# Attention's preparation rearranged: second batch's v computed inside the attention, its norm in steps between rotations, head 0's float16 pairs on other engines

## The chip, the cores and the metric

The program runs on one core of a Trainium2 chip. A core has five engines, each with its own in-order queue, which meet only at semaphores: PE (TensorE, matrix products), DVE (VectorE), ACT (ScalarE), POOL (GpSimd) and SP (SyncE, which here only issues DMAs). The metric is the device time of one execution in microseconds, with the median of several executions as the time of a kernel.

## The reference

Four layers run one after the other on an image batch x of shape (2, 128, 64, 64): an attention block, a block with deformable convolutions, three steps of a convolutional network, and a state space block. Only the first, layer 0, is touched here:

```python
# b=2, c=128, L=64*64=4096, 4 heads of ch=32 channels
xn = (xg - mean) * jax.lax.rsqrt(var + EPS)          # group norm, var with ddof=1
xi = (xn * gn_w + gn_b)                               # (b, c, L)
qkv = jnp.einsum('oc,bcl->bol', w_qkv, xi) + b_qkv[None, :, None]
q, k, v = jnp.split(jnp.transpose(qkv, (0, 2, 1)), 3, axis=2)
q = _apply_rotary(pos, q)
k = _apply_rotary(pos, k)
weight = jnp.einsum('bct,bcs->bts', qh * scale, kh * scale)   # per batch and head, L x L
weight = jax.nn.softmax(weight.astype(jnp.float16), axis=-1)
a = jnp.einsum('bts,bcs->bct', weight, vh).reshape(b, c, L)
hout = jnp.einsum('oc,bcl->bol', w_proj, a) + b_proj[None, :, None]
return (xi + hout).reshape(b, c, h, w)
```

## The kernel before

Channels lie on the 128 partitions, the 4096 pixels along the free dimension. The pixels are cut into `NBLK` = 8 blocks of `BLK` = 512. Layer 0 (function `layer0`) has two stages.

**Preparation.** x of both batches is loaded into the two tiles `q4[0]` and `q4[1]`, the rotary cosines and sines into `cs` (block by block, `load_cs`). All orders of work between `with tc.manual_schedule()` and its end are those of the program text: every engine executes its instructions in the order in which the loop issues them.

- `group_norm(b)`: eight `bn_stats` on DVE (L168), their aggregate (L170), two small matmuls with `grp` which sum over groups (L75, L82, in `group_affine`), a square root on ACT (L84), four small operations on DVE (L86 to L92), and eight ACT instructions that write the normalised image into `g.xa` (L176).
- The loop over n = 0 to 15 is batch b = n // 8, block k = n % 8. In each n, `rotated(b, k, j)` runs for q (j = 0) and k (j = 1): four PE passes into a PSUM tile `pq` (L183; three buffers), two DVE operations that multiply by cosine and sine (L185, L187, into `rt1` and `rt2`, two buffers each), an addition on POOL (L189, into `rt3`, pool `cp`, five buffers), and a store to DRAM by SP (L190, to `qd` or `kd`). The function returns the reduction of the block's largest magnitude (L191), which the loop issues one rotation later, from the list `due`.
- `values(b, k)` follows in each n: 16 PE matmuls (L199) give v of that block in PSUM (pool `psg`, two buffers). It is stored as three bfloat16 parts whose sum is the float32 value, by ACT (L204, L206, L208) and POOL (L207, L209), in `v3[b]`.
- `group_norm(1)` stands after n = 4, so batch 1 is normalised while batch 0 is still being rotated.
- At n = 10 SP loads k of head 0 (four copies, from `kd[0]`) into `q4[1]`, whose x is no longer needed, and the first two pieces of q into staging tiles (`fetch`, pool `stg`, two buffers). At n = 12 to 14 `split` turns them into float16 pairs: a float16 copy on ACT (L287), and on DVE the differences to it for some of the partitions (L289). The pairs of a head lie in `qk[0]` or `qk[1]`, which are the bytes of `q4[0]` and `q4[1]`.

After the loop the largest magnitudes become a flag (L244 to L260), each engine reads it, and a branch chooses `attend` (taken here) or `attend_any`.

**Attention** (`attend`). A unit is a batch, a head, a block `qb` of 512 queries and a block `kb` of 128 keys. Units run in groups of `GR` = 3: three score matmuls into a PSUM tile `ps` of three banks (L312; two buffers), one exp on ACT for all three (L318), and, `LAG` = 2 groups later, three matmuls that add the weighted v into `acc` (L328). `acc` comes from the pool `psa`, which has two buffers of one bank[...]. When the last key block of a query block is in, `normalise` reads `acc` on DVE (L339 reciprocal, L340 and L341 copies, L345 three products) and POOL adds the three parts (L346, L347). After the last head, `project` takes a bank of `psa` too (L354, L356). Pieces of later heads are fetched at `kb` 4 and split at `kb` 26, the copy on POOL and the differences on DVE.

Of the kernel before, what the change touches and what calls it, by code (L numbers as in the profile page):

```python
# [10 lines left out]
F32 = mybir.dt.float32  # L11
# [16 lines left out]
NH = 4  # L28
CH = P // NH
# [23 lines left out]
def interior(g, b, r0=0, rows=HW):  # L53
    return g.xa[:, b, 1 + r0 : 1 + r0 + rows, 1 : 1 + HW]
# [16 lines left out]
def group_affine(g, sm, ps_tile, mv, grp, gamma, beta, eps, unbias):  # L71


    nc = g.nc
    nc.tensor.matmul(ps_tile[:, 0:1], grp, mv[:, 0:1], start=True, stop=True)  # L75
    mg = sm.tile([P, 1], F32, name="ga_mg")
    nc.vector.tensor_copy(mg, ps_tile[:, 0:1])
    dm = sm.tile([P, 1], F32, name="ga_dm")
    nc.vector.tensor_sub(dm, mv[:, 0:1], mg)
    vt = sm.tile([P, 1], F32, name="ga_vt")  # L80
    nc.vector.scalar_tensor_tensor(vt, dm, dm, mv[:, 1:2], ALU.mult, ALU.add)
    nc.tensor.matmul(ps_tile[:, 1:2], grp, vt, start=True, stop=True)  # L82
    sd = sm.tile([P, 1], F32, name="ga_sd")
    nc.scalar.activation(sd, ps_tile[:, 1:2], AF.Sqrt, bias=eps, scale=unbias)  # L84
    rs = sm.tile([P, 1], F32, name="ga_rs")
    nc.vector.reciprocal(rs, sd)  # L86
    sc = sm.tile([P, 1], F32, name="ga_sc")
    nc.vector.tensor_mul(sc, rs, gamma)
    tm = sm.tile([P, 1], F32, name="ga_tm")
    nc.vector.tensor_mul(tm, mg, sc)  # L90
    sh = sm.tile([P, 1], F32, name="ga_sh")
    nc.vector.tensor_sub(sh, beta, tm)  # L92
    return sc, sh


def flat(ap):
    return ap.rearrange("p r w -> p (r w)")

# [1 line left out]
def layer0(g, I):  # L100
# [5 lines left out]
    nc, tc = g.nc, g.tc  # L106
    with ExitStack() as ctx:
        w = ctx.enter_context(tc.tile_pool(name="l0w", bufs=1))
        dr = ctx.enter_context(tc.tile_pool(name="l0dr", bufs=1, space=bass.MemoryType.DRAM))
        wv = w.tile([P, P], F32, name="wv")  # L110
        nc.scalar.dma_start(wv, I["wvT"])
        wpt = w.tile([P, P], F32, name="wpt")
# [14 lines left out]
        with ExitStack() as pctx:  # L127
# [20 lines left out]
            def load_cs(k):  # L148
                nc.sync.dma_start(cs[:, k], I["cossin"][:, :, k * BLK : (k + 1) * BLK])

            for k in range(4):
                load_x(0, k)
            for k in range(3):
                load_cs(k)
            for k in range(4):
                load_x(1, k)
                load_cs(3 + k)
            load_cs(7)
            bv = pw.tile([P, 1], F32, name="bv")
# [4 lines left out]
            def group_norm(b):  # L164

                st = sm.tile([P, NBLK, 6], F32, name="st")
                for k in range(NBLK):
                    nc.vector.bn_stats(st[:, k, :], q4[b][:, k * BLK : (k + 1) * BLK])  # L168
                mv = sm.tile([P, 2], F32, name="mv")
                nc.vector.bn_aggr(mv, st.rearrange("p k s -> p (k s)"))  # L170
                pg = psg.tile([P, BLK], F32, name="pm")
                n = float(P // 4 * L)
                sc, sh = group_affine(g, sm, pg, mv, grp, vec(g, "gn_w"), vec(g, "gn_b"), g.eps6, n / (n - 1.0))
                for k in range(NBLK):
                    x = img(q4[b][:, k * BLK : (k + 1) * BLK])
                    nc.scalar.activation(interior(g, b, k * RB, RB), x, AF.Identity, bias=sh, scale=sc)  # L176

            def rotated(b, k, j):

# [14 lines left out]

            def values(b, k):
                pv = psg.tile([P, BLK], F32, name="pm")
                for r in range(RB):
                    half = slice(64 * (r % 2), 64 * (r % 2) + 64)
                    nc.tensor.matmul(  # L199
                        pv[half, r // 2 * P : (r // 2 + 1) * P], g.xa[:, b, 1 + k * RB + r, 1 : 1 + HW], wv,  # L200
                        start=True, stop=True,
                    )
                v32 = sm.tile([P, 4, NH, CH], F32, name="v32")
                nc.scalar.copy(v32.rearrange("p c h d -> p (c h d)"), pv)  # L204
                dst = v3[b][:, 4 * k : 4 * k + 4]
                nc.scalar.copy(dst[:, :, :, 0:CH], v32)  # L206
                nc.gpsimd.tensor_sub(v32, v32, dst[:, :, :, 0:CH])  # L207
                nc.scalar.copy(dst[:, :, :, CH : 2 * CH], v32)  # L208
                return lambda: nc.gpsimd.tensor_sub(dst[:, :, :, 2 * CH : 3 * CH], v32, dst[:, :, :, CH : 2 * CH])  # L209

            with tc.manual_schedule():
                due = []
                group_norm(0)
                for n in range(NB * NBLK):
                    b, k = divmod(n, NBLK)
                    for j in range(2):
                        f = rotated(b, k, j)
                        for f0 in due:
                            f0()
                        due = [f]  # L220
                    due.append(values(b, k))

                    if n == 4:
                        group_norm(1)
                    if n == NBLK + 2:
                        for r in range(4):
                            nc.sync.dma_start(q4[1][r * CH : (r + 1) * CH, :], kd[0][0:CH, :])
                        first = [fetch(g, stg, qd, 0, c) for c in range(2)]
                    elif NBLK + 4 <= n < NBLK + 6:
                        for c in range(2 * (n - NBLK - 4), 2 * (n - NBLK - 4) + 2):  # L230
                            split(g, qk[0], 1, c, q4[1][:, c * PIECE : (c + 1) * PIECE], nc.scalar.copy)
                    elif n == NBLK + 6:
                        for c in range(2):
                            split(g, qk[0], 0, c, first[c], nc.scalar.copy)
                for f0 in due:
                    f0()
# [28 lines left out]
        with cond.Else():  # L265
            attend_any(g, v3, wp3, bo, qd, kd, q4)


# [12 lines left out]
    return t  # L281


def split(g, qk, j, c, t, copy):

    dst = qk[:, j, c * PIECE : (c + 1) * PIECE]
    copy(dst, t)  # L287
    for p0, p1 in ((64, 128),) if j else ((32, 64), (96, 128)):
        g.nc.vector.tensor_sub(dst[p0:p1], t[p0:p1], dst[p0:p1])  # L289


def attend(g, v3, wpt, bo, qd, kd, qk, stg):


    nc, tc = g.nc, g.tc
# [3 lines left out]
    with ExitStack() as ctx:  # L299
# [23 lines left out]
        def weigh(group, e):  # L323
            nonlocal acc
            for i, (b, h, qb, kb) in enumerate(group):
                if kb == 0:
                    acc = psa.tile([P, BLK], F32, name="acc")
                nc.tensor.matmul(acc, v3[b][:, kb, h, :], e[:, i, :], start=(kb == 0), stop=(kb == NS - 1))  # L328
# [39 lines left out]
        ]  # L368
        held, done, coming = [], [], []
        with tc.manual_schedule():  # L370
            for u in range(0, len(units), GR):
                group = units[u : u + GR]
                b, h, qb, kb = group[0]
                held.append((group, scores(group)))
                if done and 24 <= kb < 24 + GR:
                    project(*done.pop(0))
                if len(held) > LAG:
                    weigh(*held.pop(0))
                if 4 <= kb < 4 + GR:
                    coming = [(n, j, c, fetch(g, stg, (qd, kd)[j], n, c)) for n, j, c in pieces(b * NH + h, qb)]  # L380
                elif 26 <= kb < 26 + GR:
                    for n, j, c, t in coming:
                        split(g, qk[n % 2], j, c, t, nc.gpsimd.tensor_copy)
# [1636 lines left out]
```

## Time and profile before

| what | value |
|---|---|
| median of 3 runs | 5577.32 us (5575.88 to 5578.47) |
| time of the profiled execution | 5576.86 us |
| its span | 5574.9 us |
| preparation: span's start to first score matmul | 134.54 us |
| attention: first to last score group | 134.5 to 1062.6 us |
| PE busy, whole span | 4717.5 us, 85% |
| DVE busy | 4540.1 us, 81% |
| ACT busy | 4087.5 us, 73% |
| POOL busy | 3642.2 us, 65% |
| L318 exp | 683 instructions, 919.0 us busy |
| L312 and L328 | 2048 matmuls each, 554.0 and 553.6 us busy |

Engines work beside each other, so shares of busy time do not add up, and an average over the whole span says little about one stage: what a change in a stage is worth is read from the instructions of that stage and from what each of them waited for. In the lines of the profile `L185` is a line of the kernel, `out<-in` names the tile written and the tiles read, `xN` a number of instructions merged into one line, and a bracket the idle time of the engine before it with the instruction that ended it. Matmul durations overlap (they are pipelined), so their pitch, not their sum, is the time PE takes. The granted clock of PE is given as a share of full speed.

### The profile page before, as it was taken

What the parts mean: (1) busy time and instruction counts of PE and PEld (TensorE: products, weight loads), DVE (VectorE), ACT (ScalarE), POOL (GpSimd) and SP (SyncE); (2) the same over time, 40 slices, a digit from 0 to 9 for tenths busy, and PEclk for the clock granted to TensorE, in tenths of its full rate; (3) what the DMA queues carried; (4) which work ended last, traced back from release to release, by engine and by line L of the source; (5) the groups of instructions that cost most, each with busy time, mean ns of one, the idle gap of its engine ahead of it and who ended that gap; (6) DMA issues with size and microseconds to landing.
All of it is one profiled execution on the core that took longest, in us unless ns stands there. A gap on an engine that the chain in (4) does not pass through costs nothing.

```text
span 5574.9 us, 54509 instructions
## 1 busy us (share of the span) xinstructions
PE 4717.5 (85%) x17062; PEld 1756.9 (32%) x17062; DVE 4540.1 (81%) x4240; ACT 4087.5 (73%) x6282; POOL 3642.2 (65%) x1189
## 2 busy tenths in 40 slices
PE   6999999899887799878888777777787888777886
PEld 3444444344443344222222222222222222222221
DVE  6565655562245997799999999999999999999998
ACT  3999999600255212798888888888888888888886
POOL 6222222100000311699999999999999999999999
PEclk8999999999999999888887888888888887888887
DMA  4111111300464000555556555655655565565554
GB/s 155 39 46 41 36 31 38 62 1 16 79 122 78 22 0 0 125 129 142 134 127 142 138 132 127 145 127 136 151 129 130 139 142 133 128 142 136 136 134 106
DMA packets 335161, 554.27 MB, mean 99 GB/s; under 512 B 69408, under 2 KB 116016, under 8 KB 334736
## 3 DMA queue, kind: packets, MB, share of 16 engines
q1 hardware_dynamic: 333456, 549.27, 41.7%
q8 instruction: 135, 2.21, 0.2%
q10 hardware_dynamic: 1408, 1.46, 0.1%
q14 instruction: 162, 1.33, 0.1%
HBM read 461.40 MB, written 89.13 MB: 99 GB/s over the span
## 4 chain that ended last, share of the span: by engine, by line
DVE 43%; PE 35%; ACT 10%; issue 6%; DMA 2%; POOL 2%; SPq 1%; DVEq 0%; POOLq 0%; ACTq 0%
DVE db L1607 29%; DVE db L1571 10%; PE ps L312 8%; PE acc L328 8%; PE m L1161 6%; PE m L590 4%; ACT da L1593 4%; PE acd L896 2%; ACT db L1599 1%; DVE gt L1634 1%; PE m L550 1%; ACT L1458 1%; ACT u L1458 1%; PE pf L859 1%; POOL db L1617 1%
## 5 line engine op out<-in xcount | busy, mean ns | idle before, releaser
L1617 POOL TENSOR_TENSOR db<-db,c 128x2048 f32<-128x2048 f32 x512 | 2312.7, 4532 | 47.4 <-ACT hl L1612 33.0
L1593 ACT ACTIVATE da<-dd,am 128x512 f32<-128x512 f32 x2048 | 1398.3, 687 | 300.3 <-DVE db L1607 279.7
L1607 DVE TENSOR_TENSOR_SCAN db<-da,db 128x512 f32<-128x512 f32 x1376 | 1584.9, 1203 | 35.2 <-ACT db L1599 28.2
L318 ACT ACTIVATE e<-ps 128x1536 f16<-128x1536 f32 (+1 forms) x683 | 919.0, 1624 | 8.0 <-PE ps L312 8.0
L1607 DVE TENSOR_TENSOR_SCAN db<-da,hl,db 128x512 f32<-128x512 f32 x672 | 825.8, 1271 | 40.8 <-POOL db L1580 3.4
L1571 DVE TENSOR_TENSOR db<-pbc,dd 128x2048 f32<-128x2048 f32 (+1 forms) x384 | 780.7, 2033 | 31.5 <-PE pbc L1550 31.5
L1580 POOL TENSOR_TENSOR db<-b,dd 128x2048 f32<-128x2048 f32 (+1 forms) x192 | 772.7, 4025 | 13.8 <-DMA b<-bx 13.8
L1625 PE MATMUL py<-db,fold 128*32 128x512 f32 x4096 | 602.7, 674 | 153.9 <-POOL db L1617 153.7
L312 PE MATMUL ps<-q 128*128 128x512 f16 x2048 | 554.0, 379 | 4.3 <-DVE flag L260 2.7
L328 PE MATMUL acc<-e,v 128*128 128x512 f16 x2048 | 553.6, 379 | 0.1
L346 POOL TENSOR_TENSOR parts<-parts 32x512 f32<-32x512 f32 x64 | 80.5, 1257 | 707.8 <-DVE parts L345 707.8
L1599 ACT ACTIVATE db<-da,db,hl 128x1 f32<-128x1 f32 x1120 | 393.9, 352 | 148.7 <-DVE db L1571 103.6
L1212 POOL MEMSET v<- 128x256 f32 x2 | 1.1, 554 | 711.9 <-DVE b L1050 711.9
L339 DVE RECIPROCAL rec<-acc 32x512 f32<-32x512 f32 x64 | 214.9, 3358 | 257.8 <-PE acc L328 248.3
L1161 PE MATMUL m<-v,u 128*128 128x512 f32 x864 | 378.0, 600 | 43.1 <-DVE v L1104 41.5
L1518 PE MATMUL pm<-dd,ident 128*128 128x512 f32 x512 | 357.4, 836 | 2.9 <-ACT dd L1511 2.7
L1477 PE MATMUL pm<-u,wxp 128*72 128x512 f32 x256 | 186.4, 870 | 141.4 <-ACT u L1458 141.4
L1550 PE MATMUL pbc<-bc,sel 64*128 64x512 f32 x384 | 207.1, 539 | 109.2 <-DVE db L1571 108.4
L312 PEld LDWEIGHTS <-q 128*128 128x128 f16 x2048 | 197.7, 97 | 278.4 <-issue 103.8
L328 PEld LDWEIGHTS <-v 128*128 128x128 bf16 x2048 | 199.2, 97 | 248.9 <-issue 10.2
L1625 PEld LDWEIGHTS py<-db,fold 128*32 128x32 f32 x4096 | 90.0, 113 | 551.5 <-issue 326.0
L1453 PE MATMUL pm<-xn,wcs 128*128 128x512 f32 x512 | 235.3, 603 | 17.0 <-ACT xa L1652 10.5
(332 smaller groups left out, 6614.6 us busy)
## 6 DMA issues: line engine op xcount, KB each, us to landing
dd<-dx SPq DMA_DIRECT2D x1024, 256.0 KB, 6.4
dx<-dd SPq DMA_DIRECT2D x128, 512.0 KB, 5.5
c<-bx SPq DMA_DIRECT2D x1024, 64.0 KB, 2.1
b<-bx SPq DMA_DIRECT2D x512, 64.0 KB, 4.6
early<-pos SPq DMA_DIRECT2D x72, 256.0 KB, 9.8
piece<-qd SPq DMA_DIRECT2D x128, 128.0 KB, 2.8
hats<-pos SPq DMA_DIRECT2D x64, 256.0 KB, 9.7
piece<-kd SPq DMA_DIRECT2D x112, 128.0 KB, 2.7
```

The source lines that it names most:

```text
L312: nc.tensor.matmul(ps[:, i, :], t[:, 1, kb * P : (kb + 1) * P], t[:, 0, qb * BLK : (qb + 1) * BLK], start=True, stop=True,)
L318: nc.scalar.activation(e[:, :n, :], ps[:, :n, :], AF.Exp, scale=1.0 / UP**2)
L328: nc.tensor.matmul(acc, v3[b][:, kb, h, :], e[:, i, :], start=(kb == 0), stop=(kb == NS - 1))
L1161: nc.tensor.matmul(m[x], weights[j][:, dy, x, :], v[j][b][:, x, r0 : r0 + RP, :].rearrange("p r i -> p (r i)"), start=(dy == 0), stop=(dy ...
L1518: nc.tensor.matmul(ps, g.ident, S[i]["dd", hf][:, x, :], start=(x == 0), stop=(x == 1))
L1571: nc.vector.tensor_tensor(db_tile(k)[:, :, :n], G[k].pop("pb")[:, :n].unsqueeze(1).to_broadcast([P, 4, n]), S[i]["d4", hf][:, 1, :, :n], A ...
L1580: nc.gpsimd.tensor_tensor(db_tile(k)[:, :, n:], S[i]["b", ng][:, n:].unsqueeze(1).to_broadcast([P, 4, BLK - n]), S[i]["d4", hf][:, 1, :, n ...
L1593: nc.scalar.activation(da, S[i]["d4", hf][:, 0, q, :], AF.Exp, scale=am[:, hf, q, ng : ng + 1])
L1599: nc.scalar.activation(b0, da[:, first : first + 1], AF.Identity, bias=b0, scale=hl[:, hf, ng, q, :])
L1607: nc.vector.tensor_tensor_scan(d1, d0, d1, 0.0 if zero else hl[:, hf, ng, q, :], ALU.mult, ALU.add)
L1617: nc.gpsimd.tensor_mul(v, v, S[i]["c", ng].unsqueeze(1).to_broadcast([P, 4, BLK]))
L1625: nc.tensor.matmul(S[i]["y", hf][32 * q : 32 * q + 32, :], fold, G[k]["db"][:, q, :], start=False, stop=(ng == NNG - 1),)
```

## The change

Six things change; nothing outside layer 0 does.

1. The loads are issued in another order: x of batch 0, one block of cosines and sines, x of batch 1, the other seven blocks.
2. `group_norm` and `group_affine` become steps (`norm_stats`, `norm_mean`, `norm_spread`, `norm_root`, `norm_scale`, `norm_apply`). Batch 0 runs them in a row as before. Batch 1's eight stats and four small steps are issued one after each rotation (two stats before the loop, so n = 0 to 2 take six stats, n = 3 the mean and the spread, n = 4 the root and the scale), and its eight `norm_apply` four each at n = 6 and n = 7.
3. `values` runs for batch 0 alone in the loop. Batch 1's v is computed by `late_values` in the attention, in batch 0, head 1, once per query block after the group that begins at key block 12 to 14. It takes a bank of `psa`; two DVE and two POOL instructions make the three parts.
4. The load of head 0's k and first two q pieces moves from n = 10 to n = 8. Two of four pieces of k (n = 10, 11) and one of two of q (n = 12) are split in the loop, with the differences on POOL instead of DVE.
5. The remaining two pieces of k and one of q are split at the beginning of `attend`, the copy on POOL, the differences on DVE.
6. ACT loads the table of exp right after the loop (`preload_act_table_set`).

```diff
-            for k in range(3):
-                load_cs(k)
+            load_cs(0)
             for k in range(4):
                 load_x(1, k)
-                load_cs(3 + k)
-            load_cs(7)
+            for k in range(1, NBLK):
+                load_cs(k)
...
+            def norm_stats(b, k):
+                if k == 0:
+                    N[b] = sm.tile([P, NBLK, 6], F32, name="st")
+                nc.vector.bn_stats(N[b][:, k, :], q4[b][:, k * BLK : (k + 1) * BLK])
+
+            def norm_mean(b):
+                mv = N[b, "mv"] = sm.tile([P, 2], F32, name="mv")
+                nc.vector.bn_aggr(mv, N[b].rearrange("p k s -> p (k s)"))
+                N[b, "pg"] = psg.tile([P, BLK], F32, name="pm")
+                nc.tensor.matmul(N[b, "pg"][:, 0:1], grp, mv[:, 0:1], start=True, stop=True)
+
+            def norm_spread(b):
+                mv = N[b, "mv"]
+                mg, dm, vt = (sm.tile([P, 1], F32, name=f"ga_{x}") for x in ("mg", "dm", "vt"))
+                nc.vector.tensor_copy(mg, N[b, "pg"][:, 0:1])
+                nc.vector.tensor_sub(dm, mv[:, 0:1], mg)
+                nc.vector.scalar_tensor_tensor(vt, dm, dm, mv[:, 1:2], ALU.mult, ALU.add)
+                nc.tensor.matmul(N[b, "pg"][:, 1:2], grp, vt, start=True, stop=True)
+                N[b, "mg"] = mg
...
+            def norm_apply(b, k):
+                sc, sh = N[b, "to"]
+                x = img(q4[b][:, k * BLK : (k + 1) * BLK])
+                nc.scalar.activation(interior(g, b, k * RB, RB), x, AF.Identity, bias=sh, scale=sc)
...
+            def begin(c):
+                split(g, qk[0], 1, c, q4[1][:, c * PIECE : (c + 1) * PIECE], nc.scalar.copy, nc.gpsimd)
+
             with tc.manual_schedule():
...
                 due = []
-                group_norm(0)
+                steps = [lambda k=k: norm_stats(1, k) for k in range(NBLK)]
+                steps += [lambda f=f: f(1) for f in (norm_mean, norm_spread, norm_root, norm_scale)]
+                for _ in range(2):
+                    steps.pop(0)()
                 for n in range(NB * NBLK):
                     b, k = divmod(n, NBLK)
                     for j in range(2):
...
                         due = [f]
-                    due.append(values(b, k))
-
-                    if n == 4:
-                        group_norm(1)
-                    if n == NBLK + 2:
+                        if steps:
+                            steps.pop(0)()
+                    if b == 0:
+                        due.append(values(b, k))
+                    if NBLK - 2 <= n < NBLK:
+                        for k in range(4 * (n - NBLK + 2), 4 * (n - NBLK + 3)):
+                            norm_apply(1, k)
+                    elif n == NBLK:
                         for r in range(4):
                             nc.sync.dma_start(q4[1][r * CH : (r + 1) * CH, :], kd[0][0:CH, :])
                         first = [fetch(g, stg, qd, 0, c) for c in range(2)]
-                    elif NBLK + 4 <= n < NBLK + 6:
-                        for c in range(2 * (n - NBLK - 4), 2 * (n - NBLK - 4) + 2):
-                            split(g, qk[0], 1, c, q4[1][:, c * PIECE : (c + 1) * PIECE], nc.scalar.copy)
-                    elif n == NBLK + 6:
-                        for c in range(2):
-                            split(g, qk[0], 0, c, first[c], nc.scalar.copy)
+                    elif NBLK + 2 <= n < NBLK + 4:
+                        begin(n - NBLK - 2)
+                    elif n == NBLK + 4:
+                        split(g, qk[0], 0, 0, first[0], nc.scalar.copy, nc.gpsimd)
                 for f0 in due:
                     f0()
+                nc.scalar.preload_act_table_set("exp_and_others")
...
-            attend(g, v3, wpt, bo, qd, kd, qk, stg)
+            attend(g, v3, wv, wpt, bo, qd, kd, q4, qk, stg, first[1])
...
+def late_values(g, v3, pv, pool, wv, b, k):
+
+    nc = g.nc
+    value_products(g, pv, wv, b, k)
+    dst = v3[b][:, 4 * k : 4 * k + 4]
+    v = pv.rearrange("p (c h d) -> p c h d", c=4, h=NH)
+    v32 = pool.tile([P, 4, NH, CH], F32, name="v32")
+    nc.vector.tensor_copy(dst[:, :, :, 0:CH], v)
+    nc.vector.tensor_sub(v32, v, dst[:, :, :, 0:CH])
+    nc.gpsimd.tensor_copy(dst[:, :, :, CH : 2 * CH], v32)
+    nc.gpsimd.tensor_sub(dst[:, :, :, 2 * CH : 3 * CH], v32, dst[:, :, :, CH : 2 * CH])
+
+
+def split(g, qk, j, c, t, copy, less):
 
     dst = qk[:, j, c * PIECE : (c + 1) * PIECE]
     copy(dst, t)
     for p0, p1 in ((64, 128),) if j else ((32, 64), (96, 128)):
-        g.nc.vector.tensor_sub(dst[p0:p1], t[p0:p1], dst[p0:p1])
+        less.tensor_sub(dst[p0:p1], t[p0:p1], dst[p0:p1])
...
         with tc.manual_schedule():
+            split(g, qk[0], 1, 2, q4[1][:, 2 * PIECE : 3 * PIECE], nc.gpsimd.tensor_copy, nc.vector)
+            split(g, qk[0], 1, 3, q4[1][:, 3 * PIECE : 4 * PIECE], nc.gpsimd.tensor_copy, nc.vector)
+            split(g, qk[0], 0, 1, second, nc.gpsimd.tensor_copy, nc.vector)
             for u in range(0, len(units), GR):
...
                 if len(held) > LAG:
                     weigh(*held.pop(0))
+                if b == 0 and h == 1 and 12 <= kb < 12 + GR:
+                    late_values(g, v3, psa.tile([P, BLK], F32, name="acc"), sm, wv, 1, qb)
```

`value_products` holds the 16 matmuls of `values` unchanged. In the branch that is not taken here, the late v is computed before `attend_any`.

More of the change, by code (lines that the diff above doesn't have):

```diff
@@ L68, in vec @@
     return g.vecs[:, i : i + 1]
[L71 to L93, printed above, removed]
 def flat(ap):
@@ L162, in layer0 @@
                 nc.gpsimd.memset(v3[b][:, :, :, 3 * CH :], 1.0)
[L164 to L171, printed above, removed]
-                n = float(P // 4 * L)
[L173 to L176, printed above, removed]
+            N = {}
@@ new lines, in norm_spread, with norm_root @@
+            def norm_spread(b):
[6 more added lines that the diff above has]
+                N[b, "mg"] = mg
+            def norm_root(b):
+                n = float(P // 4 * L)
+                sd = N[b, "sd"] = sm.tile([P, 1], F32, name="ga_sd")
+                nc.scalar.activation(sd, N[b, "pg"][:, 1:2], AF.Sqrt, bias=g.eps6, scale=n / (n - 1.0))
@@ new lines, in norm_scale @@
+            def norm_scale(b):
+                rs, sc, tm, sh = (sm.tile([P, 1], F32, name=f"ga_{x}") for x in ("rs", "sc", "tm", "sh"))
+                nc.vector.reciprocal(rs, N[b, "sd"])
+                nc.vector.tensor_mul(sc, rs, vec(g, "gn_w"))
+                nc.vector.tensor_mul(tm, N[b, "mg"], sc)
+                nc.vector.tensor_sub(sh, vec(g, "gn_b"), tm)
+                N[b, "to"] = sc, sh
+            def norm_apply(b, k):
+                sc, sh = N[b, "to"]
+                x = img(q4[b][:, k * BLK : (k + 1) * BLK])
+                nc.scalar.activation(interior(g, b, k * RB, RB), x, AF.Identity, bias=sh, scale=sc)
@@ L196, in values @@
                 pv = psg.tile([P, BLK], F32, name="pm")
[L197 to L202, printed above, removed]
+                value_products(g, pv, wv, b, k)
                 v32 = sm.tile([P, 4, NH, CH], F32, name="v32")
@@ L209, in values @@
                 return lambda: nc.gpsimd.tensor_sub(dst[:, :, :, 2 * CH : 3 * CH], v32, dst[:, :, :, CH : 2 * CH])
+            def begin(c):
+                split(g, qk[0], 1, c, q4[1][:, c * PIECE : (c + 1) * PIECE], nc.scalar.copy, nc.gpsimd)
             with tc.manual_schedule():
+                for k in range(NBLK):
+                    norm_stats(0, k)
+                norm_mean(0)
+                norm_spread(0)
+                norm_root(0)
+                norm_scale(0)
+                for k in range(NBLK):
+                    norm_apply(0, k)
                 due = []
-                group_norm(0)
+                steps = [lambda k=k: norm_stats(1, k) for k in range(NBLK)]
+                steps += [lambda f=f: f(1) for f in (norm_mean, norm_spread, norm_root, norm_scale)]
+                for _ in range(2):
+                    steps.pop(0)()
                 for n in range(NB * NBLK):
@@ L263, in layer0 @@
         with tc.If(small > 0) as cond:
-            attend(g, v3, wpt, bo, qd, kd, qk, stg)
+            attend(g, v3, wv, wpt, bo, qd, kd, q4, qk, stg, first[1])
         with cond.Else():
+            with tc.tile_pool(name="l0vs", bufs=2) as vs, tc.tile_pool(name="l0vp", bufs=2, space=PSUM) as vp:
+                for k in range(NBLK):
+                    late_values(g, v3, vp.tile([P, BLK], F32, name="pv"), vs, wv, 1, k)
             attend_any(g, v3, wp3, bo, qd, kd, q4)
@@ L281, in fetch, with value_products @@
     return t
-def split(g, qk, j, c, t, copy):
+def value_products(g, pv, wv, b, k):
+    for r in range(RB):
+        half = slice(64 * (r % 2), 64 * (r % 2) + 64)
+        g.nc.tensor.matmul(
+            pv[half, r // 2 * P : (r // 2 + 1) * P], g.xa[:, b, 1 + k * RB + r, 1 : 1 + HW], wv,
+            start=True, stop=True,
+        )
+def late_values(g, v3, pv, pool, wv, b, k):
+    nc = g.nc
+    value_products(g, pv, wv, b, k)
+    dst = v3[b][:, 4 * k : 4 * k + 4]
[6 more added lines that the diff above has]
+def split(g, qk, j, c, t, copy, less):
     dst = qk[:, j, c * PIECE : (c + 1) * PIECE]
@@ L288, in split, with attend @@
     for p0, p1 in ((64, 128),) if j else ((32, 64), (96, 128)):
-        g.nc.vector.tensor_sub(dst[p0:p1], t[p0:p1], dst[p0:p1])
-def attend(g, v3, wpt, bo, qd, kd, qk, stg):
+        less.tensor_sub(dst[p0:p1], t[p0:p1], dst[p0:p1])
+def attend(g, v3, wv, wpt, bo, qd, kd, q4, qk, stg, second):
     nc, tc = g.nc, g.tc
@@ L382, in attend @@
                     for n, j, c, t in coming:
-                        split(g, qk[n % 2], j, c, t, nc.gpsimd.tensor_copy)
+                        split(g, qk[n % 2], j, c, t, nc.gpsimd.tensor_copy, nc.vector)
                     coming = []
```

## The prediction

> **What bounds the kernel now.** I read the groups of the first 1330 us, then the timeline engine by engine, then the windows. Layer 0 is a preparation (to 134.5 us) and an attention (to 1065 us); the change touches nothing later. DVE's timeline of the preparation (start, duration, instruction, idle before):
>
> ```profile
> 45.07 4.83 DVE L168 BATCH_NORM_STATS2 st<-q 128x6 f32<-128x512 f32 x8
> ...
> 55.96 0.75 DVE L185 SCALAR_TENSOR_TENSOR rt<-pq,vecs,cs 128x512 f32<-128x512 f32 x1 [2.58 <-PE pq L183]
> ...
> 99.75 2.36 DVE L289 TENSOR_TENSOR q<-q,q 64x1024 f16<-64x1024 f32 x2 [6.62 <-ACT q L287]
> ...
> 120.20 4.97 DVE L289 TENSOR_TENSOR q<-piece,q 32x1024 f16<-32x1024 f32 x4 [3.92 <-ACT q L287]
> ...
> 133.61 0.14 DVE L260 CAST flag<-okm 1x1 int32<-1x1 f32 x1
> ```
>
> Elsewhere a step n takes PE 4.67 us (two rotations 3.64, a `values` 1.03). Three holes stand out: the second norm (after n = 4), the split of k, the split of q. PE's timeline sizes the first:
>
> ```profile
> 58.17 1.09 PE L199 MATMUL pm<-wv,xa 128*64 128x128 f32 x16
> 59.19 3.71 PE L183 MATMUL pq<-xa,wqk 128*128 128x512 f32 x8
> ```
>
> The `values` before started at 42.85, so 10.6 us are lost there. In the attention ACT's exp is the limit (ACT's timeline):
>
> ```profile
> 142.74 366.83 ACT L318 ACTIVATE e<-ps 128x1536 f16<-128x1536 f32 x273 [0.86 <-PE ps L312]
> 510.00 14.88 ACT L318 ACTIVATE e<-ps 128x1536 f16<-128x1536 f32 x11 [0.42 <-PE ps L312]
> ```
>
> 366.83/273 = 1.344 us per group of three, without gaps; PE needs 1.30 (its pitch after each project). PE work put between groups is free only up to PE's lead: a project inserts 0.86 us (507.58 to 508.44) and ACT idles 0.42, so the lead is some 0.45 us, won back at 0.045 a group over a block's 10.7 groups.
>
> **The change, part by part.**
>
> *Loads.* x of batch 1 now precedes all but one cos/sin block. By 20 us 6.0 MB have moved (4 us windows): both x, the weights, two blocks. The second block is first used at 27.2, and the first two stats of batch 1 fill DVE's wait of 4.72 us before 22.13. Cost nothing; uncovered, the stats would be 1.2 us and late blocks a few.
>
> *Norm in steps.* A rotation takes DVE 0.66 + 0.66 + 0.59 = 1.91, a stat 0.60. With a stat after each, n = 0 to 2 run at 5.02 on DVE, over PE's 4.67: rotation (3,0) ends at 38.56, reduce and aggregate at 39.55. PE takes its queue in order, and the mean's matmul stands between the two rotations of n = 3. PE, through with (3,0) at 36.4, idles 3.2 us; DVE then idles for rotation (3,1), which could not be computed ahead. The spread's matmul repeats this. The idling also halves the clock, as windows of the trace show (columns: window, length, busy of PE, PEld, DVE, ACT, POOL, granted clock, DMA share, GB/s):
>
> ```profile
> 43.47:46.88 3.41, 0.48 (x10) 0.24 (x6) 3.41 (x7) 1.21 (x3) 3.41 (x4) 0.98 0.20 79
> 46.88:50.29 3.41, 0.00 (x0) 0.00 (x0) 3.38 (x7) 0.62 (x1) 0.63 (x1) 0.50 0.20 77
> ...
> 111.73:115.15 3.42, 1.31 (x3) 0.67 (x4) 3.39 (x6) 0.30 (x1) 1.29 (x2) 0.98 0.00 0
> 115.15:118.56 3.41, 3.41 (x20) 1.81 (x18) 1.13 (x2) 0.00 (x0) 3.41 (x3) 0.52 0.26 103
> ```
>
> The clock changes on a grid of 3.41 us; a window with little PE work is followed by one at half. Then: mean 39.6 to 40.1, rotation (3,1) at half to 43.5, DVE to 46.35, spread 46.4, `values` at half to 48.95, (4,0) to 51.4, (4,1) and `values` to 54.3, n = 5: rotation (6,0) starts at **59.0**, before at 59.19. At full clock it would be 55.7. The stats leave one hole and two others open: gain 0.2, ends -2 and 3.5.
>
> *n = 6 and 7.* `values`(6) starts at 62.6. Its third cast ends 5.26 later, as before (62.83 to 68.09), then four applies at 0.72 hold ACT to 70.8. ACT's casts of `values`(7) slip by 2.4, POOL's subtraction and the last cast follow to 73.7, four applies to 76.6. PE waits 0.3 for the first apply. SP may now load k into `q4[1]`: after the last apply and after rotation (8,1)'s store, at 76.8, before at 85.63: 8.8 earlier.
>
> *n = 8 to 15.* Without `values` a step is DVE's 3.83, not 4.67. The loads keep their size (2 MB of k, 1 MB of q pieces); from 85.63 to the first cast at 98.68 they took 13.05. So k is cast at 89.8 to 90.9. SP holds the stores back meanwhile, as before; five `rt3` buffers cover that. But POOL, in order, meets the first subtraction after t3 of (10,1), at some 83, and waits to 90.9; behind it stand the adds of n = 11, for these DVE's reduces. A POOL subtraction over 1024 columns is not in the trace: POOL's 128x512 takes 1.16, its 128x2048 4.53, hence 2.3 (ends 2.3 and 2.5; DVE 1.22). POOL: subtraction to 93.2, adds of n = 11 to 95.7, subtraction to 98.0, adds of n = 12 to 100.5, two subtractions for q to 105.1, add (13,0) to 106.3. DVE then runs alone: (14,0) to (15,1) and the last reduce end at 116.0. Tail as before, 3.54 (reduce end 131.0 to first score 134.54): first score at **119.5, gain 15.0**. With k landing 2 late, 2.5 a subtraction and the norm's -2: 9; with the norm's 3.5 and k 2 early: 20.
>
> *Exp's table.* ACT loads it at 136.15, in the path, for 1.28 us; preloaded it lies in the tail. Gain 1.2; none if it is loaded again behind the branch.
>
> *Head 0's late pieces.* Three POOL casts (1.04) and DVE subtractions (four, 1.2 to 1.9 each) at the branch. K piece 2 is ready some 3 us in, needed at block 16, fifth group, over 8 us in. Both engines idle until 155 but for this. Nothing; uncovered, up to 3. The fetches of the next pieces wait for a staging buffer, with 40 us in hand.
>
> *The late v.* Eight times in head 1 PE gets 16 matmuls, 1.02 us. They need a bank of `psa`, which has two: one collects the current block, the other is being read by the previous block's `normalise`. PE's and DVE's timelines at head 1, block 0:
>
> ```profile
> 258.42 0.81 PE L312 MATMUL ps<-q 128*128 128x512 f16 x3
> 259.07 0.81 PE L328 MATMUL acc<-e,v 128*128 128x512 f16 x3
> 259.76 0.81 PE L312 MATMUL ps<-q 128*128 128x512 f16 x3
> ```
>
> ```profile
> 255.46 3.36 DVE L339 RECIPROCAL rec<-acc 32x512 f32<-32x512 f32 x1 [8.17 <-PE acc L328]
> ...
> 259.75 2.11 DVE L345 TENSOR_TENSOR parts<-acc,rec 32x512 f32<-32x512 f32 x3
> ```
>
> Key block 12 to 14 comes three groups after the one that ends the previous block: the products stand at 259.76, the bank is read until 261.86: 2.1 us. Blocks 1 and 2 give 2.5 (275.72 against 273.2) and 2.3; with the signal, 2.4. Behind this wait stand the next scores, behind those exp. Per block 2.4 + 1.0 - 0.45 = 2.97, times 8: **23.7**. DVE's copy and subtraction (near the 1.08 of L604 and 0.68 of L345) and POOL's two fit before the next split. A project, 9 us after its `normalise`, meets no such wait.
>
> *The clock in those stalls.* The Trainium skill ("TensorE: Matmul & The Clock Gate", "HAM oscillation") warns of idle gaps above about 3.4 us; by that rule 2.4 us costs nothing. The rows say otherwise: 111.73 had 1.31 busy and halved the clock. Over the whole trace on this grid, windows at full clock with under 1.4 us of PE work were followed by half in 104 of 110 cases, 1.4 to 2.1 in 79 of 132, above that in 10 of 1007: the line is near 1.8. A gap of 2.4 falls so that one window loses over 1.6 in 77% of phases: six of eight, each a window at half, 1.7 us of PE: **10**. By the rule 0; all eight, 14. I take the rows.
>
> **Sum.** -15.0 - 1.2 + 23.7 + 10 = **+17.5** on a span of 5574.9. Its run took 5576.86; the median is 5577.32: forecast **5594.8**.
>
> **Rivals.**
> - *A, the bank is free* (another bank handed out, or released earlier): each v costs 1.0 - 0.45, 4.6 in all, no clock loss: -11.6, 5565.7, faster. For: projects share the pool and cost just 0.42 to 0.58. Against: the other bank is the accumulator. Deciding point: `normalise` over 2.4 us sooner, or two groups later placement.
> - *B, the clock holds* in gaps under one window: +7.5, 5584.8, no measurable difference. For: 53 of 132 middling windows kept it.
> - *C, the preparation gains less* (9, table reloaded) and all eight stalls halve the clock: -9 + 23.7 + 14 = +29, 5606.
> - *D, POOL's wait is harmless and the norm goes through*: gain 20 + 1.2, +12.5, 5590: same sign.
>
> **How the numbers follow.** 0.2%, 11.2 us, is about what can be told from no change. Forecast with D 0.63 (a tenth of it under 11.2), A 0.15, B 0.15, C 0.07. Slower 0.57 + 0.02 (B) + 0.07 = 0.66; faster: A, nearly all with some extra preparation gain, 0.13; same 0.21. Range 5577 to 5612: from B's lower part to C with a longer half-clock stretch, leaving A out; the forecast's own is 5587 to 5603.
>
> **What would show it.** First score near 119.5; POOL idle 7 us for ACT's cast near 83; two PE waits of 3 us at n = 3 in place of the 10.6 us hole; exp without a table load before it. In head 1 eight ACT idles of 2.9 to 4.6, PE idle for `parts`, clock at 0.5 after most. ACT idles of 0.6 there would prove A; a first score below 112 or above 126 would sink the preparation's sum.

## The result, and the profile after

The changed kernel took **5675.6 us** (5673.3 to 5679.6, six runs), against 5577.6 us for the kernel before on the same chip: a ratio of 1.0179 (95% interval 1.0169 to 1.0189). That is slower, as forecast, but by 98 us instead of 17.5, and well outside the range. Of the executions behind the medians below, one of "The kept buffer alone", 5849.8 us, fell in a slower state of the chip and is left out.

The preparation did almost what was worked out. Its lines in the changed kernel, first PE's timeline at the second norm (the columns are as before: start, duration, instruction, idle before it):

```profile
39.72 0.35 PE L149 MATMUL pm<-mv,grp 128*128 128x1 f32 x2 [3.13 <-DVE mv L147]
...
46.38 0.38 PE L157 MATMUL pm<-ga_vt,grp 128*128 128x1 f32 x2 [3.12 <-DVE ga_vt L156]
...
58.69 3.71 PE L183 MATMUL pq<-xa,wqk 128*128 128x512 f32 x8
```

The two waits of 3.1 us stand where the forecast put them, and rotation (6,0) starts at 58.69 (forecast 59.0). POOL's and ACT's timelines at the split of k and q, and at the first exp:

```profile
92.95 2.12 POOL L326 TENSOR_TENSOR q<-q,q 64x1024 f16<-64x1024 f32 x1 [6.98 <-ACT q L324]
```

```profile
91.78 1.99 ACT L324 CAST q<-q 128x1024 f16<-128x1024 f32 x2 [13.79 <-DMA q<-kd]
...
96.05 1.28 ACT L247 ACT_TABLE_LOAD   x1
123.32 1.45 ACT L355 ACTIVATE e<-ps 128x1536 f16<-128x1536 f32 x1 [25.99 <-POOL q L324]
```

POOL stands 6.98 us for ACT's cast, a subtraction takes it 2.12 us, the table of exp is loaded long before it is needed. Scores begin at 121.72 and exp at 123.32, 14.1 us earlier than before (137.44).

The loss is in the attention. The groups of the whole run (busy us and mean ns, then the idle time in front of them with its main cause), which for exp showed 8.0 us of waiting before:

```profile
L355 ACT ACTIVATE e<-ps 128x1536 f16<-128x1536 f32 (+1 forms) x683 | 922.9, 1576 | 141.6 <-PE ps L349 115.3
...
L365 PE MATMUL acc<-e,v 128*128 128x512 f16 x2048 | 567.2, 386 | 37.1 <-DVE parts L382 37.0
```

Exp as such costs nearly the same (919.0 us before), but waits 115.3 us for scores. Taken head by head from ACT's timeline, over the eight heads of both batches, the idle time within the attention is:

| head | 0 | 1 | 2 | 3 | 4 | 5 | 6 | 7 | sum |
|---|---|---|---|---|---|---|---|---|---|
| before | 1.1 | 0 | 0 | 3.3 | 0.4 | 0 | 0 | 3.3 | 8.0 |
| after | 8.1 | 43.5 | 10.0 | 24.7 | 8.3 | 8.4 | 9.0 | 3.2 | 115.3 |

The late v exists in head 1 alone, and its 43.5 us are more than the 33.7 forecast. But 71.7 us, against 8.0 before, lie in the other heads, of which the change touches only the start of head 0. The balance closes: 14.1 us won ahead, 107.3 more idle, 3.9 more exp; the last exp ends 97.4 us later (1161.82 against 1064.41).

What do the other heads wait for? The waits of the attention's stretch in the changed kernel (who waited for whom: us in all, times, longest):

```profile
DVE q L326 <- POOL q L324: 230.1, 54, 5.8
...
POOL q L324 <- DMA piece<-qd: 168.9, 30, 9.4
ACT e L355 <- PE ps L349: 115.3, 49, 8.6
...
PE acc L365 <- DVE parts L382: 37.0, 14, 4.5
```

and the same view of the kernel before:

```profile
DVE q L289 <- POOL q L287: 79.6, 25, 6.3
...
POOL q L287 <- DMA piece<-qd: 6.8, 2, 5.6
```

POOL's copies of q pieces wait for their DMA thirty times instead of twice. SP's timelines say why (x4 is one piece in four parts, x8 are two pieces). Before:

```profile
134.49 3.57 SPq L278 DMA_DIRECT2D piece<-qd  x8
143.26 1.70 SPq L278 DMA_DIRECT2D piece<-kd  x4
145.76 1.69 SPq L278 DMA_DIRECT2D piece<-qd  x4
```

After:

```profile
121.26 12.55 SPq L292 DMA_DIRECT2D piece<-qd  x8
140.20 1.70 SPq L292 DMA_DIRECT2D piece<-kd  x4
150.88 1.70 SPq L292 DMA_DIRECT2D piece<-qd  x4
158.74 1.70 SPq L292 DMA_DIRECT2D piece<-kd  x4
```

Before, the q piece of a pair is fetched 2.5 us after its k piece, into the second staging buffer. After, it is fetched 10.7 us later: **one of the two staging buffers is missing.** The tile `first[1]` is handed to `attend` as `second`; it is allocated ahead of the branch and read inside it, and from there on the pool behaves as if that buffer were never returned. That reading is what the experiments below test.

With one buffer k and q pieces take turns, and the turns close into a ring. DVE's, POOL's, PE's and ACT's timelines of one turn, in head 0:

```profile
195.61 3.36 DVE L376 RECIPROCAL rec<-acc 32x512 f32<-32x512 f32 x1
...
199.90 2.11 DVE L382 TENSOR_TENSOR parts<-acc,rec 32x512 f32<-32x512 f32 x3
204.97 1.22 DVE L326 TENSOR_TENSOR q<-piece,q 64x1024 f16<-64x1024 f32 x1 [2.96 <-POOL q L324]
211.56 2.47 DVE L326 TENSOR_TENSOR q<-piece,q 32x1024 f16<-32x1024 f32 x2 [5.36 <-POOL q L324]
214.06 3.36 DVE L376 RECIPROCAL rec<-acc 32x512 f32<-32x512 f32 x1
```

```profile
203.91 1.03 POOL L324 CAST q<-piece 128x1024 f16<-128x1024 f32 x1
210.48 1.04 POOL L324 CAST q<-piece 128x1024 f16<-128x1024 f32 x1 [5.54 <-DMA piece<-qd]
```

```profile
202.06 1.01 PE L365 MATMUL acc<-e,v 128*128 128x512 f16 x2 [4.06 <-DVE parts L382]
```

```profile
204.45 1.45 ACT L355 ACTIVATE e<-ps 128x1536 f16<-128x1536 f32 x1 [4.83 <-PE ps L349]
207.01 1.45 ACT L355 ACTIVATE e<-ps 128x1536 f16<-128x1536 f32 x1 [1.11 <-PE ps L349]
```

Follow it round: `normalise` from 195.61; POOL's additions and k's copy to 204.94; DVE's differences for k to 206.19, which free the buffer; only then SP issues q's fetch (206.22); it lands at 210.48; POOL copies, DVE subtracts to 214.03, and only then the next `normalise`, which stands behind it in DVE's queue, begins at 214.06. One turn is 18.45 us. Exp needs a query block every 14.33 us (1.344 for each of 10.67 groups). The late `normalise` keeps its bank of `acc`, so PE waits 4.06 us at 202.06, and exp 4.83 at 204.45, with a half-clock stretch about it (granted clock 0.50 from 202.40 to 205.90) and a second wait of 1.11.

### The profile page after: what moved, and what is told of

Same layout as the page of the kernel before. It is cut to its first block, busy times and chain, and to the rows that moved or that the text cites. A ratio compares the mean times of both kernels' runs of the same rounds, so it can differ in the third digit from the quotient of the medians.

```text
span 5674.4 us, 54515 instructions
## 1 busy us (share of the span) xinstructions
PE 4740.3 (84%) x17062; PEld 1766.7 (31%) x17062; DVE 4529.5 (80%) x4252; ACT 4073.3 (72%) x6255; POOL 3654.3 (64%) x1196
## 4 chain that ended last, share of the span: by engine, by line
DVE 48%; PE 28%; ACT 10%; issue 6%; DMA 3%; POOL 3%; SPq 1%; DVEq 0%; POOLq 0%; ACTq 0%
DVE db L1649 29%; DVE db L1613 10%; PE m L1203 5%; PE ps L349 5%; PE acc L365 5%; PE m L632 4%; ACT da L1635 4%; DVE rec L376 2%; PE acd L938 2%; DVE q L326 1%; DVE gt L1676 1%; ACT db L1641 1%; PE m L592 1%; DMA piece<-qd 1%; PE pf L901 1%
## 5 line engine op out<-in xcount | busy, mean ns | idle before, releaser
L355 ACT ACTIVATE e<-ps 128x1536 f16<-128x1536 f32 (+1 forms) x683 | 922.9, 1576 | 141.6 <-PE ps L349 115.3
L365 PE MATMUL acc<-e,v 128*128 128x512 f16 x2048 | 567.2, 386 | 37.1 <-DVE parts L382 37.0
L349 PE MATMUL ps<-q 128*128 128x512 f16 x2048 | 565.5, 385 | 2.5 <-issue 2.2
L326 DVE TENSOR_TENSOR q<-piece,q 32x1024 f16<-32x1024 f32 (+1 forms) x90 | 110.5, 1228 | 229.4 <-POOL q L324 228.2
```

Of the source, the lines that this page charges most:

```text
L349: nc.tensor.matmul(ps[:, i, :], t[:, 1, kb * P : (kb + 1) * P], t[:, 0, qb * BLK : (qb + 1) * BLK], start=True, stop=True,)
L355: nc.scalar.activation(e[:, :n, :], ps[:, :n, :], AF.Exp, scale=1.0 / UP**2)
```

## The experiments

All are compared with the kernel before on the same chip (5579.5 us for the first four, 5577.8 for the others). "First" and "last" are the start of the first exp and the end of the last.

**A third staging buffer.** The changed kernel with one number altered; it should give back what the kept buffer costs, if that is the cause.

```diff
-        stg = ctx.enter_context(tc.tile_pool(name="l0stg", bufs=2))
+        stg = ctx.enter_context(tc.tile_pool(name="l0stg", bufs=3))
```

> One size is changed: the staging pool has three buffers instead of two. Theory 1 (the q piece carried into the branch keeps its staging buffer for the whole attention, so k and q pieces of each later split share one buffer, and DVE's reciprocal waits behind a DMA): the exp waits outside head 1 go back to those of before (8 us in all), and head 1 keeps only the bank wait and its clock, some 27 us; with the first exp 14 us earlier than before: 5590 us, 85 under the changed kernel. Theory 2 (the late v alone, its bank wait and the halved clock, throws the later blocks out of step): three buffers change nothing, 5675 us.

Measured: 5597.2 us, ratio 1.0030 (1.0019 to 1.0041); of 98 us about 80 are gone. First 125.28, last 1080.78. SP's timeline has the pairs back:

```profile
134.91 1.70 SPq L292 DMA_DIRECT2D piece<-kd  x4
137.41 1.69 SPq L292 DMA_DIRECT2D piece<-qd  x4
```

Exp idles 35.5 us, 28.6 of them in head 1 and 6.9 elsewhere (before 8.0). ACT's timeline in head 1 now shows the late v by itself:

```profile
250.43 13.54 ACT L355 ACTIVATE e<-ps 128x1536 f16<-128x1536 f32 x10 [2.80 <-PE ps L349]
267.19 14.88 ACT L355 ACTIVATE e<-ps 128x1536 f16<-128x1536 f32 x11 [3.22 <-PE ps L349]
285.42 1.45 ACT L355 ACTIVATE e<-ps 128x1536 f16<-128x1536 f32 x1 [3.35 <-PE ps L349]
287.98 13.58 ACT L355 ACTIVATE e<-ps 128x1536 f16<-128x1536 f32 x10 [1.11 <-PE ps L349]
```

and PE's timeline the bank wait in front of each:

```profile
248.48 1.09 PE L302 MATMUL acc<-wv,xa 128*64 128x128 f32 x16 [2.03 <-DVE parts L382]
...
283.14 1.09 PE L302 MATMUL acc<-wv,xa 128*64 128x128 f32 x16 [2.25 <-DVE parts L382]
```

Five of the eight exp idles are 2.80 to 3.23, 3.02 in the mean. The other three lie at half-clock windows: two have a second idle of 1.11 behind them, and one is 4.84.

**The kept buffer alone.** The kernel before, with nothing of the change but the second q piece split at the head of `attend` (its copy on POOL instead of ACT). If the buffer is the cause, this must be slow with no late v, no new norm and no earlier load; a rival that blames the late v's contention for POOL and DVE expects no loss here.

```diff
-                        for c in range(2):
-                            split(g, qk[0], 0, c, first[c], nc.scalar.copy)
+                        split(g, qk[0], 0, 0, first[0], nc.scalar.copy)
...
-            attend(g, v3, wpt, bo, qd, kd, qk, stg)
+            attend(g, v3, wpt, bo, qd, kd, qk, stg, first[1])
...
+            split(g, qk[0], 0, 1, second, nc.gpsimd.tensor_copy)
```

> The kernel before, with one edit: the split of the second q piece of head 0 moves from the loop to the beginning of the attention, so that its staging buffer is carried through the branch. No late v. Theory 1: the exp waits of heads 0 to 6 come as in the changed kernel outside head 1 (72 us there against 8), less some 2.5 us for the split taken out of the preparation's end: 5577 + 70 = about 5647 us. Theory 2: no late v, so nothing lost: 5575 us.

Measured: 5652.8 us, ratio 1.0131 (1.0111 to 1.0152), first 136.38, last 1137.48, exp idle 79.3. Head by head it idles 7.9, 8.4, 10.2, 22.9, 8.3, 10.2, 8.1 and 3.3 us, outside head 1 close to the changed kernel. The waits of its attention have the signature of the changed kernel:

```profile
DVE q L288 <- POOL q L286: 233.6, 55, 5.6
...
POOL q L286 <- DMA piece<-qd: 170.5, 30, 7.0
...
ACT e L317 <- PE ps L311: 79.3, 42, 6.2
```

and SP's fetches alternate:

```profile
149.45 1.70 SPq L277 DMA_DIRECT2D piece<-kd  x4
163.33 1.69 SPq L277 DMA_DIRECT2D piece<-qd  x4
```

So the placement of one split costs 73 us by itself.

**The late v two or three groups later.** With three buffers, at key blocks 20 to 22 instead of 12 to 14: the bank should be free.

```diff
-                if b == 0 and h == 1 and 12 <= kb < 12 + GR:
+                if b == 0 and h == 1 and 20 <= kb < 20 + GR:
```

> Three staging buffers, and the late v after the group that begins at key block 20 to 22 instead of 12 to 14. If the rest of the late v's price is the wait for the bank that the reciprocal and products still read (2.4 us a block) and the clock that this halves, both vanish and 0.55 us a block is left: 4.6 us, total 5577 - 14 + 5 = 5568 us, and no granted clock of 0.5 in head 1. If it is the PE time of the products itself or their LDWEIGHTS, the time stays with three buffers at key block 12, near 5590 us.

Measured: 5578.6 us, ratio 0.9999 (0.9990 to 1.0007), 18.5 us better than at 12, but 10.6 above the 5568 expected. Head 1's eight idles were 0.69 to 0.70 four times, but also 1.07, 1.68, 1.69 and once 4.53, and one window at half clock was left (0.50 from 297.43 to 300.84). DVE's timeline ahead of the worst:

```profile
286.64 4.53 DVE L326 TENSOR_TENSOR q<-piece,q 64x1024 f16<-64x1024 f32 x3 [3.00 <-POOL q L324]
291.20 3.36 DVE L376 RECIPROCAL rec<-acc 32x512 f32<-32x512 f32 x1
```

The late v's own work on POOL and DVE stands, at key block 20, right ahead of the pair's split at 26; in blocks that have both, the split and then the reciprocal behind it come late, and the next bank with them. The late v spread over two heads, below, tries this.

**No late v.** Three buffers, and batch 1's `values` back in the loop; the rest of the preparation as changed. It asks what the other five parts are worth.

```diff
-                    if b == 0:
-                        due.append(values(b, k))
+                    due.append(values(b, k))
...
-                if b == 0 and h == 1 and 12 <= kb < 12 + GR:
-                    late_values(g, v3, psa.tile([P, BLK], F32, name="acc"), sm, wv, 1, qb)
```

> Three staging buffers and no late v: batch 1's v is computed in the preparation's loop again. No exp waits beyond the 8 us of before; POOL gets back two operations a step (2.2 us) behind its wait for k, so the first score comes some 11 us later than in the changed kernel, near 133 us: 5575 us, about the time before.

Measured: 5575.95 us, ratio 0.9994 (0.9985 to 1.0003), first 135.89 with the first score at 134.28, where it was before (134.54). Exp idles 6.9. The other parts alone bring the first exp 1.6 us forward, 1.3 of it the table; nearly all else that the preparation won needs v out of it.

**The norm in steps alone.** The kernel before with the new load order, the steps and the eight `norm_apply` at n = 6 and 7.

```diff
-                    if n == 4:
-                        group_norm(1)
+                        if steps:
+                            steps.pop(0)()
...
+                    if NBLK - 2 <= n < NBLK:
+                        for k in range(4 * (n - NBLK + 2), 4 * (n - NBLK + 3)):
+                            norm_apply(1, k)
```

> The kernel before with the norm alone in steps between the rotations (and the order of loads that this needs). Theory 1 (the mean's and spread's matmuls stand in PE's queue between rotations, so two waits take the place of one): PE's values of n = 5 start near 58, as before, the first score within 1 us of 134.5, the time 5577 us, no change. Rival (the stats hidden in the loop are a real gain, and the 14 us of the preparation come from here): first score near 124, 5567 us.

Measured: 5581.9 us, ratio 1.0005 (0.9997 to 1.0014): nothing. `values` of n = 5 starts at 56.92 (58.17 before), yet the first score comes at 136.84, 2.3 later. The part is worth nothing by itself, and the score is not within the 1 us that was expected. PE's timeline shows where 3.5 us go behind n = 5: at n = 8 PE waits 1.96 us for the first normalised block of batch 1 (69.31), and the two rotations behind this wait take 5.40 us instead of 3.71 (granted clock 0.50 from 71.00 to 73.00), so that `values` of n = 8 starts at 74.64 instead of 72.17.

**The late v spread over two heads.** Key block 20, three buffers, and only in the query blocks of heads 1 and 2 that bring no split (0, 5, 6, 7).

```diff
+        LATE = [(h, qb) for h in (1, 2) for qb in (0, 5, 6, 7)]
...
-                if b == 0 and h == 1 and 12 <= kb < 12 + GR:
-                    late_values(g, v3, psa.tile([P, BLK], F32, name="acc"), sm, wv, 1, qb)
+                if b == 0 and (h, qb) in LATE and 20 <= kb < 20 + GR:
+                    late_values(g, v3, psa.tile([P, BLK], F32, name="acc"), sm, wv, 1, LATE.index((h, qb)))
```

> Three staging buffers; the late v in heads 1 and 2, in query blocks 0, 5, 6 and 7, which split no pieces, at key block 20 to 22. Theory (at key block 20 a wait for the bank is left only where POOL's late work pushes a split behind it and with it the next reciprocal, blocks 2 to 5): eight exp waits of 0.7 us, none longer, 5.5 us instead of 11.7, no clock of 0.5: 5572 us. Rival (any bank taken out of turn costs a wait now and then): 5578 us as with key block 20 in head 1.

Measured: 5570.1 us, ratio 0.9985 (0.9979 to 0.9992): faster than before. ACT's timeline has all eight at the same small price:

```profile
324.38 13.54 ACT L355 ACTIVATE e<-ps 128x1536 f16<-128x1536 f32 x10 [0.69 <-PE ps L349]
338.61 14.88 ACT L355 ACTIVATE e<-ps 128x1536 f16<-128x1536 f32 x11 [0.69 <-PE ps L349]
```

That is 5.5 us for the eight, in place of the 28.6 at key block 12 and 11.7 at key block 20 of head 1.

**The norm's products one rotation later.** As the last, with the two small matmuls as steps of their own, behind the next rotation's products, so that PE no longer stands in front of DVE's aggregate.

```diff
-                steps += [lambda f=f: f(1) for f in (norm_mean, norm_spread, norm_root, norm_scale)]
+                steps += [lambda f=f: f(1) for f in (norm_mean, norm_mean_product, norm_spread, norm_spread_product, norm_root, norm_scale)]
```

> The same, and the mean's and the spread's matmuls issued one rotation after the DVE work that they need, so that PE has a rotation between. Theory 1: the two DVE waits of 3.7 and 5.1 us at n = 3 and 4 shrink to under 1, everything behind moves up, first score 6 to 7 us earlier than in the kernel without this edit: 5565 us. Rival (POOL's and DMA's chain behind n = 8 sets the end, not the norm): first score unchanged.

Measured: 5565.6 us, ratio 0.9978 (0.9968 to 0.9988), first 120.85. DVE's two idles for PE there are 1.63 and 3.14 us, in the run just above 3.99 and 6.30; under 1 was expected. The first score comes 3.6 us earlier (119.25, before the edit 122.86) instead of 6 to 7, and the two intervals overlap.

**The split later, the load on ACT's queue.** As the last, with the loads of k and of the first q pieces issued by ACT, the two subtractions of k at n = 12 and 13, those of q at n = 14.

```diff
-                            nc.sync.dma_start(q4[1][r * CH : (r + 1) * CH, :], kd[0][0:CH, :])
-                        first = [fetch(g, stg, qd, 0, c) for c in range(2)]
-                    elif NBLK + 2 <= n < NBLK + 4:
-                        begin(n - NBLK - 2)
-                    elif n == NBLK + 4:
+                            nc.scalar.dma_start(q4[1][r * CH : (r + 1) * CH, :], kd[0][0:CH, :])
+                        first = [fetch(g, stg, qd, 0, c, nc.scalar) for c in range(2)]
+                    elif NBLK + 4 <= n < NBLK + 6:
+                        begin(n - NBLK - 4)
+                    elif n == NBLK + 6:
```

> The same, and head 0's k and q pieces loaded from ACT's queue instead of SP's, and split at n = 12, 13 and 14 instead of 10, 11 and 12, when k has landed. Theory: POOL's wait of 7 us and DVE's of 8 at n = 11 vanish, SP's stores are not held back, the first score comes 8 us earlier again: 5557 us. Rival (POOL's subtractions, 8.6 us, now at the end, stand in front of the last additions and give it back): first score the same or later.

Measured: **5562.8 us**, ratio 0.9974 (0.9963 to 0.9984), the fastest of all, 15.0 us below the kernel before; 5557 was expected. First 113.00, last 1046.12. POOL still meets k too early, for 5.61 us instead of 7.38 in the run just above:

```profile
91.45 2.12 POOL L332 TENSOR_TENSOR q<-q,q 64x1024 f16<-64x1024 f32 x1 [5.61 <-ACT q L330]
```

The first exp came 7.9 us sooner than in the run just above, the median only 2.8; the two intervals overlap, so what the last step adds is open.

## Why the prediction was wrong

**The failed step.** Under "Head 0's late pieces" the prediction put "Nothing; uncovered, up to 3", and: "The fetches of the next pieces wait for a staging buffer, with 40 us in hand." It took the wait for one of a few microseconds at the start. The buffer does not come back during the attention: the piece that is read inside the branch keeps it, and all later pairs of all heads go through one. The range had no case for it either. Its size is shown from both sides: 73 us when it is put into the kernel before, about 80 when it is taken out of the changed one. The 7 us between lie in head 1, where exp idles 43.5 us with the kept buffer and the late v together, but 8.4 and 28.6 with each alone. That the tile's allocation ahead of the branch is what keeps the buffer is read from SP's alternating fetches and from the third buffer's effect; a second q piece fetched again inside the branch was not tried.

**The late v was sized well.** With the third buffer the bank waits were 2.03 to 2.55 us (2.4 in the sum) and an exp idle without the clock's part 3.02 (2.97). Rival A, the free bank, is the kernel with the late v spread: 0.69 each, 5.5 in all, against 4.6 worked out; the deciding point it named, two groups later, was right only where no split follows.

**The clock was oversized.** Six of eight stalls were to halve it, for 10 us; in the kernel with three buffers three did. A stall that did not halve it and one that did, in the windows view on the clock's own grid (window, length, busy of PE, of its weight loads PEld, of DVE, ACT, POOL, granted clock, DMA share, GB/s):

```profile
264.04:267.45 3.41, 2.21 (x22) 1.45 (x23) 2.15 (x4) 0.26 (x1) 2.52 (x2) 1.00 0.00 0
267.45:270.86 3.41, 3.41 (x18) 1.52 (x17) 0.42 (x2) 3.41 (x3) 2.85 (x4) 1.00 0.00 0
...
281.10:284.51 3.41, 1.37 (x18) 1.06 (x19) 2.15 (x4) 0.97 (x1) 1.99 (x2) 1.00 0.02 5
284.51:287.93 3.42, 3.42 (x10) 1.18 (x8) 1.15 (x2) 1.45 (x1) 2.55 (x4) 0.50 0.00 0
```

The eight idles sum to 28.6; eight of 3.02 make 24.1, so the clock cost 4.4, about 1.5 for each halved window (1.7 forecast). What was off is the count. In the window of each stall with the least PE work, PE was busy 0.86, 1.37 and 1.42 us where the clock was halved, and 1.50 to 2.20 in the five where it held. So PE's work in a window does tell, as the prediction had it, but only four of the stalls brought a window under its line of 1.8, and one of these (1.50) kept the clock; how eight gaps fall on the grid is chance. The Trainium skill ("TensorE: Matmul & The Clock Gate", "HAM oscillation") warns of idle gaps above about 3.4 us; the trace shows shorter ones at work: PE stood 2.25 us ahead of 283.14 and the clock halved.

**The preparation was nearly right.** The norm in steps: gain 0.2 forecast, 0.5 at rotation (6,0), and nothing in the median when made alone. At n = 8 PE waited 1.99 us, not 0.3, for the first normalised block of batch 1 (70.08), and a half-clock window followed (0.50 from 71.10 to 74.52); SP issued the load of k at 78.86 instead of 76.8, and it landed for ACT's cast at 91.78 instead of 89.8; POOL's subtraction took 2.12 instead of 2.3; first score 121.72 instead of 119.5. The table of exp was worth 1.3: from first score to first exp 2.90 us before, 1.60 after. Together 14.1 of 16.2.

**The sum without the failed step.** With the third buffer the first exp came 12.2 us earlier, exp idled 28.6 in head 1, and the last exp ended 16.4 later; the median rose by 17.7. The forecast of 17.5 was thus that of the change with a third staging buffer. Its misses, 4.0 too much won in the preparation and 5.6 too much lost to the clock, nearly cancel, so that 17.5 and 17.7 lie this close is luck; and though the sign came right, 80 of the 98 us came from a wait that the prediction put at nothing.

## What to carry over

When a tile of a rotating pool is passed into code that lives on (a branch, a long loop), ask when its buffer comes back before asking how long its first user takes: with one of two buffers gone, stages that were apart become one ring, and every engine's queue behind it is late. Look for that in the issue times of the transfers: alternating single issues, where pairs stood before, are a buffer count. And work moved into another stage should be placed by what follows it on each of its engines' queues; the same eight pieces of v cost 28.6, 11.7 or 5.5 us of exp's time by their place alone.

## What was not expected of the hardware

- A PE gap of 2.03 us (ahead of 354.77) was followed by a half clock, one of 2.46 (ahead of 319.21) was not: with three buffers the windows held 1.42 and 1.50 us of PE work. Neither gap nor work was varied by itself.
- Operations of DVE on 128x1 took 0.15 to 0.22 us mostly, but some 0.67 to 1.1. In the changed kernel the three long ones of the second norm each end with a POOL operation that runs beside them, to 0.02 us. DVE's and POOL's timelines:

```profile
55.40 1.12 DVE L168 TENSOR_TENSOR ga_sc<-ga_rs,vecs 128x1 f32<-128x1 f32 x1
56.55 1.08 DVE L169 TENSOR_TENSOR ga_tm<-ga_mg,ga_sc 128x1 f32<-128x1 f32 x1
```

```profile
55.23 1.27 POOL L189 TENSOR_TENSOR rt<-rt,rt 128x512 f32<-128x512 f32 x1
56.45 1.16 POOL L202 TENSOR_TENSOR v<-v,v 128x512 f32<-128x512 f32 x1
```

The third is L155 (45.41 to 46.08; POOL to 46.06). All three read two tiles, neither in PSUM; a copy from PSUM beside the same POOL operation took 0.15 (45.23). In the kernel before, POOL was idle at this place and the same two multiplications took 0.16 each (52.83, 53.02). This is read from the traces and was not tested.

- The code behind the attention is the same in all these kernels, yet from the last exp to the span's end the profiled runs took 4510.0 to 4516.2 us. And with the preparation's code alike, the first exp stood at 123.3 to 125.3 in the changed kernel and in the three with only its staging buffer and its late v altered. A single profiled run can't show gains of a few microseconds; the stage's own times can.
